# Reordering the last eight row blocks of a one-core graph-attention and layer-norm kernel

## The chip, the cores and the metric

The kernel runs on one core of a Trainium2 chip. The metric is the device time of one execution in microseconds. Six runs of the kernel before took 236.86 to 239.29 us, with a median of 237.13.

## The reference

`x` has 4096 rows of 512 numbers, `adj` 4096 rows of 4096, and `W` maps 512 features to 4 heads of 512. With the head count H = 4, what is computed is:

```
ht      = (x @ W) split into heads
e       = leaky_relu(src_i + dst_j) + adj[i, j]      for each head
h_prime = mean over heads of softmax_j(e) @ ht
out     = layernorm(x + h_prime)                     eps = 1e-5
```

The entries of `adj` reach 1e9 and most are zero, so in each row the largest entry leads by far more than the attention scores can make up. The softmax is then one at the column of that entry and zero elsewhere, and the row's result is `layernorm(x[i] + x[col(i)] @ mean of the heads' W)`. The kernel computes this, and beside it a test that every row's lead is large enough: a bound on the scores from the norms of x and of the weight vectors, compared with the gap between the largest and the second largest entry. The number of rows that fail is counted; if it is not zero, a general path follows, which these inputs don't enter.

## The kernel before

The rows are handled in 32 blocks of 128 (NB = 32), row `p * 32 + ib` being partition p of block ib. `BEHIND` is 24, `LATE` is 28, `KB` is 4 (512 features in four parts of 128). The order of the work is written out by hand: each engine executes its instructions in the order in which the program issues them, and the framework adds the semaphore waits between engines.

For each block the steps are:

- SyncE's queue loads the block's adjacency (2 MB). VectorE reduces it to 64 segment maxima (L163) and finds the largest segment (L170, L172). GpSimd fetches that segment with an indirect DMA (L176). VectorE finds the column in it (L192, L198), and GpSimd gathers the rows of x at these columns (`gather_rows`, L186). For block 31 VectorE searches the whole adjacency row instead (`find_column_in_row`, L206, 128 x 4096).
- `turn`: TensorE transposes the gathered rows in four parts into PSUM (L213), and ScalarE copies them to SBUF as `yt` (L215).
- `residual` adds the block's own rows of x to the PSUM accumulator through a product with the identity (L221). `products(ib, lo, hi)` adds the products of parts lo to hi-1 with the mean weights (L228). An fp32 product shows in the profile as two passes.
- The layer norm has two forms. `stats`, `rstd` and `finish`: two passes with sums on ScalarE (L250, L252), three small operations on GpSimd (L255 to L257) and a scaling on ScalarE (L261). Or `moments`, `factor` and `normalise`: VectorE takes mean and variance (L281, L285), ScalarE the root (L287), VectorE the reciprocal (L290; with `shift` also minus mean times reciprocal, L292) and the scaling (L297). `finish` can follow `factor` with `shift`.
- `row_norm`: ScalarE sums the squares of the block's x (L235), for the bound.

In the loop over the blocks these steps overlap. Blocks 24 to 27 are treated apart: their products alone are copied to a buffer (`put_by`, L241), and x is added later (`add_x`, L244, on GpSimd or VectorE), because their x is loaded only after the last adjacency. Block 31 is worked in two halves of 256 columns with an accumulator each (`residual_in_halves` L266, `products_of_half` L270, `stats_of_half` L304, `finish_in_halves`).

What follows the loop, L456 to L522, is the end of the kernel, and is what the change rewrites. In it stand, in the order of the program: the row norms of the last blocks; the stores of finished blocks; the column search of 30 and 31; the x of 24 to 27; residual, products and norm of 28 to 31; and the test. The test is `bound(0)` (the largest row norm `xm` on VectorE, L367, turned into a row by TensorE, L369), `bound(1)` (its maximum `xg`, L371, and root on ScalarE, L372), `bound(2)` (spread over the partitions by TensorE, L375), `bound(3)` and `test` (eight small VectorE operations, L377 to L390), `count` (a product with ones on TensorE, L394) and `report` (three VectorE operations, L398 to L401). `find_inner` (L192) takes the eight largest of a fetched segment.

The part of the end that sets the order between TensorE and VectorE reads:

```python
    residual(LATE)
    products(LATE, KB - 1, KB)
    residual_in_halves(NB - 1)
    turn(NB - 3)
    residual(NB - 3)
    products(NB - 3, 0, KB - 1)
```

Of the kernel before, what the change touches and what calls it, by code (L numbers as in the profile page):

```python
# [66 lines left out]
def leading_rows(ctx, tc, x, adj, W, a, out, ident, v, n_bad, any_bad):  # L67
# [141 lines left out]
    def turn(ib):  # L209
        y = y_t.pop(ib)  # L210
        tp = psum.tile([P, KB, P], F32, name="tp", bufs=2)
        for kb in range(KB):
            nc.tensor.transpose(tp[:, kb, :], y[:, ts(kb, P)], ident)  # L213
        yt = yt_of[ib] = rows.tile([P, KB, P], F32, name="yt")
        nc.scalar.copy(yt, tp)  # L215

    def residual(ib):
        start = ib not in o_ps
        if start:
            o_ps[ib] = psum.tile([P, D], F32, name="o")  # L220
        nc.tensor.matmul(o_ps[ib], ident, hold[:, ib, :], start=start, stop=False)  # L221

    def products(ib, lo=0, hi=KB):
        start = ib not in o_ps
        if start:
            o_ps[ib] = psum.tile([P, D], F32, name="o")
        for kb in range(lo, hi):
            nc.tensor.matmul(  # L228
                o_ps[ib], yt_of[ib][:, kb, :], w_sum[:, kb, :],
                start=(start and kb == 0), stop=(kb == KB - 1),  # L230
            )

    def row_norm(ib):
        sq = rows.tile([P, D], F32, name="sq")
        nc.scalar.activation(sq, hold[:, ib, :], AF.Square, accum_out=xx[:, ib : ib + 1])  # L235
# [7 lines left out]
    def add_x(engine, ib):  # L243
        engine.tensor_add(hold[:, ib, :], hold[:, ib, :], o_ps["by"][:, ib - BEHIND, :])  # L244
        o_ps[ib] = hold[:, ib, :]

    def stats(ib):
        o, i = o_ps[ib], slice(ib, ib + 1)
        sq = rows.tile([P, D], F32, name="sq")
        nc.scalar.activation(sq, o, AF.Identity, scale=-1.0 / D, accum_out=nm[:, i])  # L250
        sq = rows.tile([P, D], F32, name="sq")
        nc.scalar.activation(sq, o, AF.Square, bias=nm[:, i], accum_out=sd[:, i])  # L252
# [6 lines left out]
    def finish(ib):  # L259
        i = slice(ib, ib + 1)  # L260
        nc.scalar.activation(hold[:, ib, :], o_ps.pop(ib), AF.Identity, bias=nm[:, i], scale=sd[:, i])  # L261

    def residual_in_halves(ib):
        o_ps[ib] = [psum.tile([P, D // 2], F32, name="o") for _ in range(2)]
        for k, o in enumerate(o_ps[ib]):
            nc.tensor.matmul(o, ident, hold[:, ib, ts(k, D // 2)], start=True, stop=False)  # L266
# [10 lines left out]
    def moments(ib):  # L277

        if ib < NB - 1:
            st = small.tile([P, nc.vector.BN_STATS_DIM], F32, name="st", bufs=2)  # L280
            nc.vector.bn_stats(st, o_ps[ib])  # L281
        else:
            st = halves_st
        mv = mean_var[ib] = small.tile([P, nc.vector.BN_AGGR_DIM], F32, name="mv", bufs=3)
        nc.vector.bn_aggr(mv, st)  # L285
        r = rt[ib] = sd[:, ib : ib + 1]
        nc.scalar.activation(r, mv[:, 1:2], AF.Sqrt, bias=eps)  # L287
# [8 lines left out]
    def normalise(ib, o, columns=slice(0, D)):  # L296
        nc.vector.tensor_scalar(  # L297
            hold[:, ib, columns], o, mean_var[ib][:, 0:1], rt[ib], op0=OP.subtract, op1=OP.mult
        )
# [63 lines left out]
    def bound(part):  # L363

        if part == 0:
            xm = once.tile([P, 1], F32, name="xm")
            nc.vector.tensor_reduce(xm, xx, axis=AX.X, op=OP.max)  # L367
            px = of_bound[0] = psum.tile([1, P], F32, name="px", bufs=1)
            nc.tensor.transpose(px, xm, ident)  # L369
        elif part == 1:  # L370
            nc.vector.tensor_reduce(xg, of_bound[0], axis=AX.X, op=OP.max)  # L371
            nc.scalar.activation(xg, xg, AF.Sqrt)  # L372
        elif part == 2:
            pb = of_bound[2] = psum.tile([P, 1], F32, name="px", bufs=1)
            nc.tensor.matmul(pb, ones[0:1, :], xg, start=True, stop=True)  # L375
        else:
            nc.vector.tensor_mul(lead_by, of_bound[2], vn)  # L377
            nc.vector.tensor_scalar(lead_by, lead_by, 1.05, 110.0, op0=OP.mult, op1=OP.add)
# [3 lines left out]
    def test():  # L382
        a1 = top[:, :, 0]
        nc.vector.tensor_tensor(gap, top[:, :, 1], inner[:, :, 1], op=OP.max)
        size = once.tile([P, NB], F32, name="size")
        nc.vector.scalar_tensor_tensor(size, a1, -1.0, a1, op0=OP.mult, op1=OP.max)
        nc.vector.tensor_sub(gap, a1, gap)
        nc.vector.tensor_scalar(size, size, -(2.0 ** -22), lead_by, op0=OP.mult, op1=OP.subtract)
        nc.vector.scalar_tensor_tensor(gap, gap, 0.9999, size, op0=OP.mult, op1=OP.add)
        nc.vector.tensor_scalar(gap, gap, 0.0, None, op0=OP.is_gt)  # L390

    def count():
        pg = psum.tile([1, NB], F32, name="px", bufs=1)
        nc.tensor.matmul(pg, ones[:, 0:1], gap, start=True, stop=True)  # L394
        return pg
# [57 lines left out]
            finish(t - FINISH)  # L453
            finish(t - FINISH + 1)

    for ib in range(BEHIND, LATE + 2):  # L456
        row_norm(ib)
    for ib in range(0, 2 * Q, Q):
        store(nc.sync, ib, Q)
# [1 line left out]
        store(nc.sync, ib, 2)  # L461
    find_column(NB - 2)
    add_x(nc.gpsimd, BEHIND)
    add_x(nc.gpsimd, BEHIND + 1)
    find_column_in_row(NB - 1)
    add_x(nc.gpsimd, BEHIND + 2)
    residual(LATE)
    products(LATE, KB - 1, KB)
    residual_in_halves(NB - 1)
    turn(NB - 3)  # L470
    residual(NB - 3)
    products(NB - 3, 0, KB - 1)
    row_norm(NB - 2)
    row_norm(NB - 1)
    moments(LATE)
    for ib in range(BEHIND, NB):
        find_inner(ib)
    bound(0)
    products(NB - 3, KB - 1, KB)
    stats(BEHIND)  # L480
    factor(LATE)
    normalise(LATE, o_ps.pop(LATE))
    bound(1)
    turn(NB - 2)
    bound(2)
    add_x(nc.vector, LATE - 1)
    stats(BEHIND + 1)
    moments(LATE - 1)
    products(NB - 2, 0, 2)
    bound(3)  # L490
    test()
    pg = count()
    products(NB - 2, 2, KB - 1)
    stats(BEHIND + 2)
    rstd(slice(BEHIND, BEHIND + 2))
    rstd(slice(BEHIND + 2, BEHIND + 3))
    moments(NB - 3)
    report(pg)
    turn(NB - 1)
    factor(LATE - 1, shift=True)  # L500
    factor(NB - 3)
    normalise(NB - 3, o_ps.pop(NB - 3))
    finish(BEHIND)
    finish(BEHIND + 1)
    products(NB - 2, KB - 1, KB)
    products_of_half(NB - 1, 0)
    products_of_half(NB - 1, 1)
    nc.vector.tensor_add(hold[:, NB - 2, :], o_ps[NB - 2], hold[:, NB - 2, :])
    o_ps[NB - 2] = hold[:, NB - 2, :]
    moments(NB - 2)  # L510
    stats_of_half(NB - 1, 0)
    factor(NB - 2)
    normalise(NB - 2, o_ps.pop(NB - 2))
    finish(BEHIND + 2)
    finish(BEHIND + 3)
    stats_of_half(NB - 1, 1)
    moments(NB - 1)
    factor(NB - 1, shift=True)
    finish_in_halves(NB - 1)
    for ib, n in ((NB - 4, 1), (NB - 3, 1), (BEHIND, 2), (NB - 2, 1), (BEHIND + 2, 2)):  # L520
        store(nc.sync, ib, n)
    store(nc.sync, NB - 1, 1)  # L522

# [152 lines left out]
```

## Time and profile before

| what | value |
|---|---|
| median of six runs | 237.13 us |
| the profiled execution | 237.11 us |
| its span | 235.6 us |
| TensorE busy | 198.5 us, 84% |
| VectorE busy | 186.6 us, 79% |
| ScalarE busy | 111.7 us, 47% |
| GpSimd busy | 101.3 us, 43% |
| DMA | 97.73 MB, mean 415 GB/s |
| VectorE, segment maxima (L163) | 68 instructions, 146.0 us |
| TensorE, products (L228) | 248 passes, 117.0 us |
| TensorE, residuals (L221) | 52 passes, 28.5 us |

The span is the time from the first to the last instruction of the program; what the measured time has beyond it, 1.5 us here, lies around it. Shares of busy time are averages over the whole span. They say little of the end of the kernel, where the adjacency has arrived and a few engines hand work to one another: there the chain of waits, the timeline and the windows are to be read. In a line of the timeline the first number is the start, the second the busy time, then engine, line, operation, what it writes from what, and in brackets the idle time before it and what ended that.

### The profile page before, as it was taken

What the parts mean: (1) busy time and instruction counts of PE and PEld (TensorE: products, weight loads), DVE (VectorE), ACT (ScalarE), POOL (GpSimd) and SP (SyncE); (2) the same over time, 40 slices, a digit from 0 to 9 for tenths busy, and PEclk for the clock granted to TensorE, in tenths of its full rate; (3) what the DMA queues carried; (4) which work ended last, traced back from release to release, by engine and by line L of the source; (5) the groups of instructions that cost most, each with busy time, mean ns of one, the idle gap of its engine ahead of it and who ended that gap; (6) DMA issues with size and microseconds to landing.
All of it is one profiled execution on the core that took longest, in us unless ns stands there. A gap on an engine that the chain in (4) does not pass through costs nothing.

```text
span 235.6 us, 2500 instructions
## 1 busy us (share of the span) xinstructions
PE 198.5 (84%) x683; PEld 102.8 (44%) x683; DVE 186.6 (79%) x302; ACT 111.7 (47%) x267; POOL 101.3 (43%) x215
## 2 busy tenths in 40 slices
PE   0198959999999999999959999697899968799990
PEld 0034526456656556656434443242443433245460
DVE  2735875589869995999579979898799899989772
ACT  2002012155757557474726464546464645137782
POOL 1112232415427462646352655464365564548130
PEclk9999799999999999999985999999799999999999
DMA  6999999999999999999999999999999999999995
GB/s 232 436 441 410 445 417 440 415 440 417 431 436 410 429 428 446 420 420 440 417 431 437 420 437 423 430 417 433 426 439 411 419 426 419 419 423 420 417 361 214
DMA packets 13697, 97.73 MB, mean 415 GB/s; under 512 B 2152, under 2 KB 2152, under 8 KB 7792
## 3 DMA queue, kind: packets, MB, share of 16 engines
q1 hardware_dynamic: 10080, 88.08, 88.6%
q0 software_dynamic: 3584, 9.44, 10.1%
q8 instruction: 6, 0.10, 0.2%
q14 instruction: 11, 0.09, 0.1%
q10 hardware_dynamic: 16, 0.02, 0.0%
HBM read 89.15 MB, written 8.39 MB: 414 GB/s over the span
## 4 chain that ended last, share of the span: by engine, by line
POOL 33%; issue 33%; DMA 18%; PE 9%; DVE 3%; POOLq 1%; ACT 1%; SPq 1%
DMA adj_t<-in_adj_dram 15%; POOL lead L176 11%; POOL y L186 10%; PE o L228 5%; POOL sd L256 4%; DMA y<-in_x_dram,col 3%; POOL start L181 2%; POOL col L200 2%; POOL row L174 2%; DVE seg L163 2%; PE o L270 2%; POOL sd L255 1%; POOL nm L257 1%; PE tp L213 1%; PE o L221 1%
## 5 line engine op out<-in xcount | busy, mean ns | idle before, releaser
L163 DVE TENSOR_REDUCE seg<-adj_t 128x32 f32<-128x2048 f32 (+1 forms) x68 | 146.0, 2150 | 35.1 <-DMA adj_t<-in_adj_dram 34.6
L228 PE MATMUL o<-w_sum,yt 128*128 128x512 f32 x248 | 117.0, 612 | 1.0 <-ACT yt L215 1.0
L228 PEld LDWEIGHTS o<-w_sum,yt 128*128 128x128 f32 x248 | 45.4, 194 | 56.1 <-issue 44.5
L215 ACT COPY yt<-tp 128x512 f32<-128x512 f32 x32 | 18.8, 588 | 46.7 <-PE tp L213 43.9
L176 POOL DMA_INDIRECT lead<-in_adj_dram,row x32 | 32.3, 1010 | 14.2 <-POOL row L174 14.2
L186 POOL DMA_INDIRECT y<-in_x_dram,col x32 | 30.9, 965 | 16.0 <-POOL col L200 15.5
L318 PE MATMUL o<-hold,ident 128*128 128x512 f32 x32 | 18.9, 745 | 15.2 <-DMA hold<-in_L_gnn_W_dram 15.2
L213 PE MATMUL tp<-ident,y 128*128 128x128 f32 x128 | 20.3, 283 | 11.8 <-DMA y<-in_x_dram,col 11.8
L221 PE MATMUL o<-hold,ident 128*128 128x512 f32 x52 | 28.5, 631 | 0.5 <-DMA hold<-in_x_dram 0.5
L213 PEld LDWEIGHTS tp<-ident,y 128*128 128x128 f32 x128 | 15.1, 145 | 24.7 <-issue 23.5
L200 POOL TENSOR_TENSOR col<-start,within 128x1 uint32<-128x1 uint32 x31 | 5.9, 190 | 45.5 <-DVE within L198 45.5
L336 ACT COPY wt<-tp 128x512 f32<-128x512 f32 x16 | 9.2, 587 | 32.3 <-PE tp L334 27.7
L174 POOL TENSOR_TENSOR row<-at,first 128x1 uint32<-128x1 uint32 x32 | 6.1, 189 | 39.3 <-DVE at L172 39.3
L235 ACT ACTIVATE sq<-hold 128x512 f32<-128x512 f32 x32 | 19.8, 619 | 0.0
L342 PEld LDWEIGHTS pv<-at_d,wt 128*128 128x128 f32 x128 | 16.3, 191 | 6.8 <-ACT wt L336 3.5
L318 PEld LDWEIGHTS o<-hold,ident 128*128 128x128 f32 x32 | 7.3, 239 | 24.5 <-POOL row L174 11.1
L319 ACT ACTIVATE w_sum<-o 128x512 f32<-128x512 f32 x4 | 2.4, 598 | 31.5 <-PE o L318 31.5
L261 ACT ACTIVATE hold<-o,nm,sd 128x512 f32<-128x512 f32 x24 | 17.2, 770 | 0.0
L252 ACT ACTIVATE sq<-o,nm 128x512 f32<-128x512 f32 x24 | 16.5, 687 | 0.8
L342 PE MATMUL pv<-at_d,wt 128*128 128x2 f32 x128 | 15.3, 244 | 0.6 <-ACT wt L336 0.6
L250 ACT ACTIVATE sq<-o 128x512 f32<-128x512 f32 x24 | 14.6, 607 | 0.0
L334 PEld LDWEIGHTS tp<-ident,hold 128*128 128x128 f32 x64 | 7.9, 142 | 6.9 <-issue 6.9
(85 smaller groups left out, 138.2 us busy)
## 6 DMA issues: line engine op xcount, KB each, us to landing
adj_t<-in_adj_dram SPq DMA_DIRECT2D x27, 2048.0 KB, 32.5
hold<-in_x_dram SPq DMA_DIRECT2D x7, 1024.0 KB, 31.6
adj_t<-in_adj_dram SPq DMA_DIRECT2D x6, 1024.0 KB, 30.7
out_dram<-hold SPq DMA_DIRECT2D x10, 512.0 KB, 11.9
adj_t<-in_adj_dram SPq DMA_DIRECT2D x8, 512.0 KB, 13.6
hold<-in_L_gnn_W_dram SPq DMA_DIRECT2D x4, 1024.0 KB, 8.2
out_dram<-hold SPq DMA_DIRECT2D x2, 1024.0 KB, 15.7
hold<-in_x_dram SPq DMA_DIRECT2D x2, 512.0 KB
```

Source lines behind the costliest of these rows:

```text
L163: nc.vector.tensor_reduce(seg_of[ib][:, ts(k, S // n)], adj_t[ib][:, ts(k, N // n)].rearrange("p (s e) -> p s e", e=E), axis=AX.X, op=OP.max,)
L176: nc.gpsimd.indirect_dma_start(out=lead, out_offset=None, in_=adj_segs, in_offset=bass.IndirectOffsetOnAxis(ap=row[:, :1], axis=0),)
L186: nc.gpsimd.indirect_dma_start(out=y, out_offset=None, in_=x, in_offset=bass.IndirectOffsetOnAxis(ap=col[:, :1], axis=0),)
L213: nc.tensor.transpose(tp[:, kb, :], y[:, ts(kb, P)], ident)
L215: nc.scalar.copy(yt, tp)
L221: nc.tensor.matmul(o_ps[ib], ident, hold[:, ib, :], start=start, stop=False)
L228: nc.tensor.matmul(o_ps[ib], yt_of[ib][:, kb, :], w_sum[:, kb, :], start=(start and kb == 0), stop=(kb == KB - 1),)
L235: nc.scalar.activation(sq, hold[:, ib, :], AF.Square, accum_out=xx[:, ib : ib + 1])
L252: nc.scalar.activation(sq, o, AF.Square, bias=nm[:, i], accum_out=sd[:, i])
L261: nc.scalar.activation(hold[:, ib, :], o_ps.pop(ib), AF.Identity, bias=nm[:, i], scale=sd[:, i])
L318: nc.tensor.matmul(o, ident, hold[:, w_at + kb * H + h, :], start=(h == 0), stop=(h == H - 1))
L342: nc.tensor.matmul(pv[:, kb, h : 2 * H : H], wt[:, k, :], at_d[:, k, h : 2 * H : H], start=(k == 0), stop=(k == KB - 1),)
```

## The change

The end of the kernel is rewritten in its order, and two steps change their engine:

- Block 28 has no residual on TensorE. VectorE adds its x to the finished products, with a new function `add_x_to_products`, which block 30 already had written out.
- Block 26 has its mean and variance from VectorE (`moments`, and `factor` with `shift`) instead of ScalarE and GpSimd (`stats`, `rstd`). GpSimd adds block 26's x before block 25's, and both after the gather of block 31.
- Turn 29 is issued before the half residuals of 31. Turn 30 is issued before residual 29 and the last product of 29, turn 31 after the first product of 30 and before the other three.
- The steps of the bound, the test and the count stand at other places among these. The maxima of the fetched segments are taken in two groups of four. Row norm 29 follows the copy of turn 29.
- The x of block 27 is added after the report, with its moments later still.
- The store of blocks 26 and 27 is issued ahead of block 30's.
- The tile `mv` has six buffers instead of three.

Four lines are added ahead of the end, so its line numbers in the changed kernel are higher by four than those above.

```diff
+    def add_x_to_products(ib):
+        nc.vector.tensor_add(hold[:, ib, :], o_ps[ib], hold[:, ib, :])
+        o_ps[ib] = hold[:, ib, :]
...
-        mv = mean_var[ib] = small.tile([P, nc.vector.BN_AGGR_DIM], F32, name="mv", bufs=3)
+        mv = mean_var[ib] = small.tile([P, nc.vector.BN_AGGR_DIM], F32, name="mv", bufs=6)
...
-    for ib in range(BEHIND, LATE + 2):
+    for ib in range(BEHIND, LATE + 1):
         row_norm(ib)
...
     find_column(NB - 2)
     add_x(nc.gpsimd, BEHIND)
-    add_x(nc.gpsimd, BEHIND + 1)
     find_column_in_row(NB - 1)
     add_x(nc.gpsimd, BEHIND + 2)
-    residual(LATE)
+    add_x(nc.gpsimd, BEHIND + 1)
     products(LATE, KB - 1, KB)
+    turn(NB - 3)
     residual_in_halves(NB - 1)
-    turn(NB - 3)
-    residual(NB - 3)
     products(NB - 3, 0, KB - 1)
-    row_norm(NB - 2)
-    row_norm(NB - 1)
+    for ib in range(LATE + 1, NB):
+        row_norm(ib)
+    add_x_to_products(LATE)
     moments(LATE)
-    for ib in range(BEHIND, NB):
+    stats(BEHIND)
+    moments(BEHIND + 2)
+    bound(0)
+    for ib in range(BEHIND, LATE):
         find_inner(ib)
-    bound(0)
-    products(NB - 3, KB - 1, KB)
-    stats(BEHIND)
     factor(LATE)
     normalise(LATE, o_ps.pop(LATE))
+    factor(BEHIND + 2, shift=True)
+    turn(NB - 2)
     bound(1)
-    turn(NB - 2)
+    residual(NB - 3)
     bound(2)
-    add_x(nc.vector, LATE - 1)
+    products(NB - 3, KB - 1, KB)
+    for ib in range(LATE, NB):
+        find_inner(ib)
     stats(BEHIND + 1)
-    moments(LATE - 1)
-    products(NB - 2, 0, 2)
+    rstd(slice(BEHIND, BEHIND + 2))
     bound(3)
     test()
+    products(NB - 2, 0, 1)
     pg = count()
-    products(NB - 2, 2, KB - 1)
-    stats(BEHIND + 2)
-    rstd(slice(BEHIND, BEHIND + 2))
-    rstd(slice(BEHIND + 2, BEHIND + 3))
+    finish(BEHIND + 2)
+    turn(NB - 1)
     moments(NB - 3)
     report(pg)
-    turn(NB - 1)
-    factor(LATE - 1, shift=True)
+    add_x(nc.vector, LATE - 1)
     factor(NB - 3)
     normalise(NB - 3, o_ps.pop(NB - 3))
     finish(BEHIND)
     finish(BEHIND + 1)
-    products(NB - 2, KB - 1, KB)
+    moments(LATE - 1)
+    products(NB - 2, 1, KB)
     products_of_half(NB - 1, 0)
     products_of_half(NB - 1, 1)
-    nc.vector.tensor_add(hold[:, NB - 2, :], o_ps[NB - 2], hold[:, NB - 2, :])
-    o_ps[NB - 2] = hold[:, NB - 2, :]
+    factor(LATE - 1, shift=True)
+    finish(LATE - 1)
+    add_x_to_products(NB - 2)
     moments(NB - 2)
     stats_of_half(NB - 1, 0)
     factor(NB - 2)
     normalise(NB - 2, o_ps.pop(NB - 2))
-    finish(BEHIND + 2)
-    finish(BEHIND + 3)
     stats_of_half(NB - 1, 1)
...
-    for ib, n in ((NB - 4, 1), (NB - 3, 1), (BEHIND, 2), (NB - 2, 1), (BEHIND + 2, 2)):
+    for ib, n in ((NB - 4, 1), (NB - 3, 1), (BEHIND, 2), (BEHIND + 2, 2), (NB - 2, 1)):
         store(nc.sync, ib, n)
```

## The prediction

> **What bounds the kernel now.** I read four views in this order. First the page's second part: the DMA row is full from the second slice to the last but one, so the body streams the adjacency at the DMA's speed. The change touches nothing there; only what follows the last adjacency rows, from about 209 us, can move. Second the chain of waits over that stretch, because it tells which engine sets the end:
>
> ```profile
> 209.42 0.63 PE tp L213 x4
> 210.05 3.57 PE o L228 x8
> 213.62 0.86 PE o L221 x2
> 214.48 0.86 PE o L228 x2
> ...
> 221.58 0.02 issue
> 221.60 0.59 ACT yt L215
> 222.20 0.04 issue
> 222.24 1.99 PE o L228 x4
> ...
> 226.73 3.55 PE o L270 x16
> 230.28 0.02 issue
> 230.30 0.44 DVE halves_st L304
> ```
>
> Columns: start, length, what. From 209.42 to 230.28 the chain stays on TensorE but for one stop of 0.65 us, the copy of block 30's turned rows at 221.60. Each 512-wide fp32 product or residual is two passes, 0.86 us. After 230.30 comes a serial tail of moments, root, reciprocal, scaling and last store, which the change leaves alone.
>
> Third the timeline of GpSimd and VectorE there, for the operations that are moved:
>
> ```profile
> 211.37 4.42 DVE L206 FIND_INDEX8 col<-top,adj_t 128x8 uint32<-128x4096 f32 x1
> ...
> 213.56 2.51 POOL L244 TENSOR_TENSOR hold<-hold,adj_t 128x512 f32<-128x512 f32 x2
> ...
> 216.55 0.97 POOL L186 DMA_INDIRECT y<-in_x_dram,col  x1 [0.48 <-issue]
> 217.54 1.28 POOL L244 TENSOR_TENSOR hold<-hold,adj_t 128x512 f32<-128x512 f32 x1
> ...
> 218.53 0.18 DVE L367 TENSOR_REDUCE xm<-xx 128x1 f32<-128x32 f32 x1 [0.93 <-ACT sq L235]
> ...
> 219.99 0.27 PE L369 MATMUL px<-ident,xm 128*1 128x128 f32 x1
> ```
>
> The gather of block 31 cannot start before VectorE's search ends at 215.79; the add of block 26's x (L244 at 217.54) stands behind that gather on GpSimd. Fourth the one-microsecond windows: DMA moves about 418 GB/s up to 226 us and 201 to 432 after it, so the last stores run almost at the DMA's pace too. The (26,27) store is issued at 230.2 and takes 3.4 us to land.
>
> [...] all of these rows run in the written order. [...] the add from PSUM (L508) took 692. [...] normalise took 0.81 from PSUM and 0.55 from SBUF.
>
> **The change, part by part.** Line numbers are those of before.
>
> 1. Block 28's residual leaves TensorE: minus 2 passes, 0.86 us on the chain. Its add goes to VectorE, 0.69 + 0.04 us, right after the search, where VectorE had 0.93 us idle before xm; its normalise now reads SBUF, 0.26 shorter.
> 2. Turn 29 is ahead of the two half residuals (4 x 0.215 = 0.86), which hide the 0.59 us copy as residual 29 did. It would start at 214.32; the queue's wait for gather 29 ended at 214.1, so 0.2 us of cover is left. Products 29 (three, six passes) then run 215.61 to 218.26 instead of 217.34 to 219.99. So far TensorE is 1.7 us ahead.
> 3. GpSimd: gather 31 no longer waits for the second add. Search end 215.79, release 0.04, then 0.27 to 0.51 as the other gathers show: start 216.10 to 216.34, take 216.22 (before 216.55). Add 26 follows: 217.21 to 218.49. Add 25 moves behind it, to 219.8; its readers on ScalarE come at 221.5.
> 4. Block 26's moments move to VectorE (0.73 + 0.18) and **add a wait**: VectorE stands at 217.33 and waits for add 26 until 218.53. Queued behind it: xm, four maxima, block 28's scaling, all of the bound. Moments end at 219.4, xm runs 219.35 to 219.53 (the 218.53 it had was a wait for row norms, which now end at 217.6). ScalarE loses the two passes of 26 (1.56 us) and GpSimd one rstd (about 1.1); both had idle time, so nothing is won there.
> 5. TensorE reaches the first bound product (L369) at 218.26 and waits for xm until 219.60: **1.34 us idle**, because turn 30, residual 29 and product 29 stand behind it. Turn 30 starts at 219.73 (before 220.96); gather 30 was issued at 212.57 and took 6.7 us, so it is there at 219.3. Its copy (0.65 with waits) is now hidden by residual 29, which ends at 221.03.
> 6. Second bound product: VectorE after xm does four maxima (4 x 0.126), reciprocal 28, normalise 28 (0.55 + 0.2), factor 26 (0.35), then xg at 220.93, 0.28; ScalarE's root to 221.43; product at 221.47. TensorE idle 0.44 us. Then product 29 and one of 30, 221.75 to 223.54, while VectorE's maxima and test (1.28 after the product's end at 221.87) end at 223.2: no wait at count. Count at 223.54 (before 224.15).
> 7. Turn 31 at 223.69 (before 225.27). Gather 31 is due at 216.22 + 6.7 = 222.9. Behind it now stand three products of 30 (6 x 0.4285 = 2.57) and the halves: 223.69 + 0.43 + 2.57 = 226.70, halves 16 passes, 226.70 + 15 x 0.2155 + 0.38 = 230.31 (before 230.26). The copy of 31 (0.59) is hidden by the products.
> 8. VectorE's tail: report, add 27 (0.67), scaling 29 (0.81), moments and factor of 27, add and moments of 30 (0.69, 0.69, 0.18), first half's moments (0.43), scaling 30 (0.55). Laid end to end with ScalarE's roots between, scaling 30 ends at 230.5 to 230.75 (before 229.65), so the second half's moments start then, against 230.30: **plus 0.2 to 0.45 us**. ScalarE's finish of 24 to 27 is done by 228.8.
> 9. Stores: (26,27) goes ahead of 30, issued near 228.8 instead of 230.2; 30 near 230.7 instead of 229.7. Both precede the last, issued near 232.7 (before 232.32). Three more mv buffers add no instruction: nothing.
>
> Sum on TensorE: minus 0.86 (residual), minus about 0.4 (wait for copy 30 that showed as idle), plus 1.34 and 0.44 of new idle time; minus about 0.45 of what the first bound product, turn 30, second product and count had lost to their own starts: about zero. VectorE's tail adds 0.2 to 0.45, middle 0.35. The profiled execution took 237.11 us with a span of 235.6; the median of the runs is 237.13, the same. Predicted: 237.13 + 0.35 = 237.5 us.
>
> Unknown costs. Gather 31's dispatch: 0.12 us either side, one for one. Landing of gathers: 6.7, 6.8 in this stretch, median 7.9 and longest 9.5 over the run; below 7.4 it is free. GpSimd's add beside VectorE's work: 1.28 in all three rows; I take it, with 1.2 and 1.5 as bounds. Moments of 26 gain if ScalarE's relief reaches the tail; the finish of 27 is before the last scaling anyhow, so between 0 and minus 0.2.
>
> **The rivals.** *A (likeliest, 0.70):* as above; with its bounds minus 0.3 to plus 1.0, so 236.8 to 238.1.
>
> *B, the wait at the first bound product is small and the end moves up (0.17).* For it: TensorE's work really shrinks by 0.86 plus the 0.37 us idle before 222.24, which would end the halves at 229.0. Against: the search, gather, add, moments order is fixed by three FIFO queues. Even then the gain is cut: the (26,27) store landed at 230.2 + 3.4 = 233.6 behind stores that were queued, and 0.25 MB more take 0.6 us at 418 GB/s, so the last store can hardly land before 234.2; it now lands about 1 us before the span's end, at 234.6. Gain 0.4: 236.7 us.
>
> *C, slower: gather 31 lands late (0.13).* Turn 31 was at 225.27, 8.7 us after its gather's issue; now it is at 223.69, 7.5 after, and 2.57 us of block 30's products stand behind it on the in-order TensorE. Any landing beyond 7.4 us delays the end one for one. At the longest of this trace, 9.5, that is 2.0 on top of 0.35: 239.5 us. Against it: the two gathers nearest in time took 6.7 and 6.8.
>
> That the change doesn't do what it says is not likely: by the queues, bound, count and copy of 31 do come sooner (0.4, 0.6 and 1.6 us by my schedule); what does not come sooner is the end.
>
> **How the numbers follow.** About 1%, 2.4 us, is what a measurement of this kernel can tell from no change (its own six runs lie between 236.86 and 239.29). A and B are wholly within it. C passes it only at its far end. With the runs' own spread of 2.4 us upwards: faster 0.02, same 0.88, slower 0.10. The range takes B's 236.7 and A with its bounds, and part of C: 236.6 to 238.9, leaving out about 0.15.
>
> **What would show it.** VectorE's wait of about 1.2 us ended by GpSimd's add, before a 128x512 moments; TensorE idle more than 1 us before the first bound product; turn 31 near 223.7; last half product ending near 230.3; a second-half moments start at 230.5 or later, with scaling 30 just before it. I am wrong if that first wait is under 0.5 us, if turn 31 waits for its gather, or if the last store's issue is before 232.

## The result and the profile after

| | before | after |
|---|---|---|
| median of all runs | 237.07 us (71 runs, 236.56 to 239.71) | 238.46 us (33 runs, 237.73 to 239.41) |
| ratio to before, 95% interval | 1 | 1.0038 (1.002 to 1.0055) |
| profiled execution | 237.11 us | 237.93 us |
| its span | 235.6 us | 236.4 us |
| last store issued | 232.32 | 232.50 |
| its last part landed after the issue | 2.31 us | 2.94 us |

The trace records 16 landings for the last store, called its parts here, from 1.84 to 2.31 us after the issue in before and from 1.85 to 2.94 in after. The ratio compares fast executions and is what the text goes by (the medians alone stand 0.6% apart): 0.38% of 237.1 us is 0.9 us, with 0.5 to 1.3 as its interval. That is slower, by less than the 1% that counts as a change here, and within the predicted range. The predicted 0.4 us (237.5 against 237.13) lies just under the interval.

The timeline of after, in the stretch where before was read (start, length, engine, line, operation, and in brackets the idle time ahead of it with what ended it):

```profile
211.03 4.42 DVE L206 FIND_INDEX8 col<-top,adj_t 128x8 uint32<-128x4096 f32 x1
...
216.21 0.96 POOL L186 DMA_INDIRECT y<-in_x_dram,col  x1 [1.96 <-issue]
...
218.51 0.69 DVE L285 BATCH_NORM_STATS2 st<-hold 128x6 f32<-128x512 f32 x1 [1.52 <-POOL hold L244]
...
219.54 0.27 PE L373 MATMUL px<-ident,xm 128*1 128x128 f32 x1 [1.51 <-DVE xm L371]
...
221.39 0.29 PEld L379 LDWEIGHTS px<-xg,ones 1*128 1x128 f32 x2 [0.78 <-ACT xg L376]
221.39 0.38 PE L379 MATMUL px<-xg,ones 1*128 1x1 f32 x2
...
223.76 0.66 PE L213 MATMUL tp<-ident,y 128*128 128x128 f32 x4
```

The new wait is there: VectorE stands 1.52 us until GpSimd's add of block 26 ends, and TensorE behind it 1.51 us until xm. The second bound product itself shows no idle time, but its weight load (PEld) waited for ScalarE's root, which was done at 221.33. Turn 31 is at 223.76. The search of block 31, 215.79 at its end before, ended at 211.03 + 4.42 = 215.45 here. That is 0.34 us sooner with nothing changed ahead of it; times of the two traces are therefore compared from the search's end too. The gather of 31 starts at 216.21, which is 0.76 after that end. Before, it was 216.55 - 215.79 = 0.76 as well.

The chain of waits of after (start, length, what):

```profile
217.20 1.28 POOL hold L244
218.48 0.02 issue
218.51 0.70 DVE st L285
219.21 0.02 issue
219.24 0.18 DVE mv L289
219.42 0.08 DVE xm L371
219.50 0.04 issue
219.54 0.28 PE px L373
219.83 0.12 issue
219.95 0.63 PE tp L213 x4
...
229.92 0.55 DVE hold L301
230.47 0.02 issue
230.48 0.44 DVE halves_st L308
```

Where before had TensorE alone, the chain now runs GpSimd's add, VectorE's moments, xm, the bound product, turn 30. At its end the second half's moments (L308, at 230.48) follow directly on the scaling of block 30 (L301) instead of the last product. The last product ended at 230.45, so TensorE and VectorE come to the end together. From the search's end the moments stand at 230.48 - 215.45 = 15.03, against 230.30 - 215.79 = 14.51 before: the computation ends 0.52 us later. That is no chance of one execution: the same two figures come back in e4 and e5 below (15.03, the arithmetic of after) and in e6 and e8 (14.51, that of before). On the traces' own clocks the last store goes out only 0.18 later, since this execution's search was 0.34 sooner.

The other 0.63 us of the spans' difference lie **behind the last instruction of the kernel's arithmetic**. The DMA rate over 3.2 us from the issue of the last store, in 40 slices of 80 ns, first before, then after:

```profile
GB/s 307 52 103 0 102 0 102 51 51 0 179 384 410 410 410 410 384 410 205 77 0 205 0 0 0 0 0 0 0 0 0 0 0 0 0 0 0 0 0 0
```

```profile
GB/s 51 51 51 51 0 0 0 0 0 0 179 333 486 384 384 358 384 358 231 52 102 0 26 26 51 26 26 26 26 26 0 0 0 0 0 0 0 0 0 0
```

The bulk moves in the same slices, 0.8 to 1.5 us after the issue. The single 205 of before, at 1.7 us, is two 8 KB packets. Then after shows eight slices at 26 to 51 GB/s, to 2.4 us, where before is empty: a few engines are still at work. The completions agree: 14 of the 16 parts of the store land by 1.98 us after its issue in both, the last two at 2.26 and 2.31 before and at 2.89 and 2.94 after.

What else goes over the DMA engines there? The program ends with `flag = nc.values_load(any_bad[0:1, 0:1], ...)` (L61) and a branch on it, in every engine's instruction stream. Of the queues, the "instruction" one moves two packets of 8 KB in this stretch, in both traces. The loads of the flag, on VectorE's and ScalarE's sequencers (shortest, median, longest in ns, then start in us), first before, then after:

```profile
L61 DVEq TENSOR_LOAD <-any_bad x1: 806/806/806, 231.5 to 231.5; - x1
L61 ACTq TENSOR_LOAD <-any_bad x1: 656/656/656, 231.7 to 231.7; - x1
```

```profile
L61 DVEq TENSOR_LOAD <-any_bad x1: 537/537/537, 231.7 to 231.7; - x1
L61 ACTq TENSOR_LOAD <-any_bad x1: 477/477/477, 231.9 to 231.9; - x1
```

Both start 0.77 and 0.58 us ahead of the last store's issue in both kernels. In before the loads end 0.04 and 0.07 us after it, in after 0.23 and 0.11 us ahead of it. The two 8 KB packets on the instruction queue, called fetches here, follow the loads: at 1.70 and 1.71 us after the issue in before, at 1.02 and 1.64 in after, where the first took 766 ns instead of 309. That the branch brings them about is the author's reading; the traces show the order alone. Why are the loads shorter in after? The one-microsecond windows (stretch, its length, the five engines' busy times, then TensorE's clock, DMA share and GB/s), before and then after:

```profile
231.00:232.00 1.00, 0.00 (x0) 0.00 (x0) 0.63 (x3) 0.57 (x2) 0.00 (x0) 1.00 1.07 432
232.00:233.00 1.00, 0.00 (x0) 0.00 (x0) 0.15 (x1) 0.29 (x1) 0.00 (x0) 1.00 0.49 201
```

```profile
231.00:232.00 1.00, 0.00 (x0) 0.00 (x0) 0.60 (x4) 0.38 (x2) 0.00 (x0) 1.00 0.73 287
232.00:233.00 1.00, 0.00 (x0) 0.00 (x0) 0.33 (x1) 0.48 (x1) 0.00 (x0) 1.00 0.12 45
```

In before the (26,27) store, issued at 230.2, keeps the DMA at 432 GB/s from 231 to 232, while the flag is loaded. In after that store went out at 228.69 and that of block 30 alone at 230.49, so the DMA drains before the last store comes: 287 GB/s in the first window, 45 in the second. **Theory:** an idle DMA gives a short load, an early branch, and fetches that meet the last store. **Rival:** the loss is in the arithmetic's order (the new wait and VectorE's tail), and the landing is chance.

### The profile page after: what moved, and what is told of

Its sections match the earlier page's. It is cut to its first block, busy times and chain, and to the rows that moved or that the text cites. A ratio compares the mean times of both kernels' runs of the same rounds, so it can differ in the third digit from the quotient of the medians.

```text
span 236.4 us, 2495 instructions
## 1 busy us (share of the span) xinstructions
PE 198.2 (84%) x681; PEld 102.6 (43%) x681; DVE 187.7 (79%) x307; ACT 110.8 (47%) x264; POOL 100.2 (42%) x212
## 4 chain that ended last, share of the span: by engine, by line
POOL 32%; issue 30%; DMA 16%; PE 15%; DVE 3%; ACT 1%; POOLq 1%; SPq 0%
DMA hold<-in_L_gnn_W_dram 11%; POOL lead L176 10%; POOL y L186 10%; PE o L228 7%; POOL sd L260 3%; DMA y<-in_x_dram,col 3%; PE o L322 2%; DMA adj_t<-in_adj_dram 2%; POOL start L181 2%; POOL col L200 2%; PE pv L346 2%; POOL row L174 2%; PE tp L213 2%; PE o L221 1%; POOL hold L244 1%
## 5 line engine op out<-in xcount | busy, mean ns | idle before, releaser
L228 PE MATMUL o<-w_sum,yt 128*128 128x512 f32 x248 | 115.0, 606 | 0.7 <-ACT yt L215 0.7
L322 PE MATMUL o<-hold,ident 128*128 128x512 f32 x32 | 20.9, 813 | 14.8 <-DMA hold<-in_L_gnn_W_dram 14.8
L221 PE MATMUL o<-hold,ident 128*128 128x512 f32 x50 | 27.4, 631 | 0.0
L322 PEld LDWEIGHTS o<-hold,ident 128*128 128x128 f32 x32 | 8.1, 264 | 25.3 <-POOL row L174 11.0
L254 ACT ACTIVATE sq<-o 128x512 f32<-128x512 f32 x24 | 14.6, 608 | 0.0
```

The lines of the kernel that those rows point to most:

```text
L228: nc.tensor.matmul(o_ps[ib], yt_of[ib][:, kb, :], w_sum[:, kb, :], start=(start and kb == 0), stop=(kb == KB - 1),)
L322: nc.tensor.matmul(o, ident, hold[:, w_at + kb * H + h, :], start=(h == 0), stop=(h == H - 1))
```

## The experiments

Kernels of one batch shared a chip and its runs of before: (e1, e2, e3, e5), (e4, e7, e8, e9), (e6, e11, e12, e13). Ratios are to before.

**e1: the wait that holds the bound back.** In after, xm and the four maxima go ahead of block 26's moments.

```diff
-    moments(BEHIND + 2)
     bound(0)
     for ib in range(BEHIND, LATE):
         find_inner(ib)
+    moments(BEHIND + 2)
```

> The changed kernel with one step moved: the largest row norm xm and four of the maxima go ahead of block 26's moments on VectorE. Theory 1 (VectorE's wait for GpSimd's add of block 26 holds back xm, and with it TensorE): TensorE's idle time before the first bound product falls from 1.5 us to about 0.1, but gather 30, which landed at 219.8, then ends the wait before turn 30, so TensorE still idles 0.8 to 1.5 us there and the kernel gains no more than 0.3 us on the changed one. Rival (VectorE's tail sets the end, TensorE has slack): idle time moves in the same way and the end doesn't move at all, within 0.2 us of the changed kernel. Rival (the wait alone is the whole loss): the kernel falls by 0.9 us or more, to the kernel before.

Measured: 1.0052 (1.0034 to 1.007). The 1.51 us of idle time before the first bound product is gone, but the kernel is no faster for it. TensorE then waited 0.31 us for gather 30, 0.93 before the second bound product and, as its timeline shows, for gather 31:

```profile
225.54 0.63 PE L213 MATMUL tp<-ident,y 128*128 128x128 f32 x4 [0.18 <-DMA y<-in_x_dram,col]
```

From the search's end, the last half product ended after 14.62 us instead of 15.0: the 1.5 us of waiting was worth 0.4. The last part of the last store landed 3.38 us after its issue, more than in after.

**e2: e1, and block 29 finished ahead of turn 30.**

```diff
-    turn(NB - 2)
-    bound(1)
     residual(NB - 3)
-    bound(2)
     products(NB - 3, KB - 1, KB)
+    turn(NB - 2)
+    bound(1)
+    bound(2)
```

> As the run before, and residual 29 and the last product of 29 go ahead of turn 30 again, which fills the time in which TensorE would wait for gather 30. Theory 1: no idle time over 0.4 us on TensorE between 218 and 220; the halves' last product ends near 229.3 instead of 230.4, and the second half's moments start at 229.9 to 230.4, then bound by VectorE. Time 0.3 to 0.8 us under the changed kernel. Rival (VectorE's tail): the last product ends a microsecond earlier and the time stays within 0.2 us of the changed kernel. Rival (the last store is what was lost): the time depends on where the store's issue falls against the instruction fetch, and does not follow TensorE.

Measured: 1.0057 (1.0033 to 1.0082). The waits moved again (0.20 us for gather 30, 0.77 before the second bound product, 0.35 before the count), the end stayed at 14.6. The store landed after 3.14 us. Neither order of TensorE's queue repairs the loss.

**e3: block 28's x on VectorE alone, in before.**

```diff
-    residual(LATE)
...
+    nc.vector.tensor_add(hold[:, LATE, :], o_ps[LATE], hold[:, LATE, :])
+    o_ps[LATE] = hold[:, LATE, :]
     moments(LATE)
```

> The kernel before with one part of the change: block 28's x is added on VectorE and its residual leaves TensorE; all else stands as before. Theory 1 (TensorE's work sets the end of the kernel before): the last product ends 0.7 to 0.9 us sooner than 230.26, VectorE's second-half moments start near 229.6, and the time falls by 0.4 to 0.8 us under the kernel before. Rival (the stores' DMA sets the end): the last product ends as much sooner, but the last store lands no more than 0.4 us sooner. Rival (VectorE is the bound): no gain, since the add costs it 0.7 us.

Measured: 1.0003 (0.9981 to 1.0025). The profile shows the residual's 0.86 us: from the start of turn 28 the halves end after 20.11 us instead of 20.84, and the last store goes out after 22.17 instead of 22.89. But one of its parts landed late, 2.77 us after the issue, so 0.46 of the 0.73 us are given back there. Contrary to what the expectation of e9 says below, no fetch stands ahead of that part: its 2 KB packets run on until 2.17 us after the issue, and a fetch starts at 2.18. The (26,27) store's own last part had landed only 1.89 us after that issue.

**e5: more engine work behind the last store, in after.** One 128x512 copy on ScalarE and one 128x512 add on VectorE, whose results nothing reads, were to hold the branch back.

```diff
+    nc.scalar.copy(rows.tile([P, D], F32, name="sq"), w_sum[:, 0, :])
+    nc.vector.tensor_add(rows.tile([P, D], F32, name="wt"), w_sum[:, 1, :], w_sum[:, 2, :])
```

> The changed kernel with work added: after their last instruction ScalarE copies 128x512 once more and VectorE adds 128x512 once more, into buffers that nothing reads, so that their branch to the program's end comes 0.6 us later. Theory of the fetch (in the profiled run of the changed kernel an instruction fetch of 8 KB on the DMA engines starts 0.2 us after the last store's first packets and holds back a part of them by 0.7 us; before, it starts after them): the last store lands about 2.3 us after its issue instead of 2.9, and the kernel gets faster by 0.3 to 0.6 us although it does more. Rival (the fetch is chance, or of no weight): the time stays the same or grows by up to 0.6 us.

Measured: 1.005 (1.003 to 1.007). The loads didn't move: they again start 0.77 and 0.58 us ahead of the store's issue and take 0.54 and 0.47. The fetches came 1.04 and 1.05 us after the issue and took 829 and 756 ns, and the store landed after 3.35 us. VectorE's sequencer loads the flag at 232.3, while its engine still has operations queued: VectorE is busy for 0.88 us of the window from 232 to 233 and for 0.50 us of the next. So the edit failed in its purpose and told something else: the work added at the end did not delay the load, nor the fetches after it.

**e4: before's order of the last stores, in after.**

```diff
-    for ib, n in ((NB - 4, 1), (NB - 3, 1), (BEHIND, 2), (BEHIND + 2, 2), (NB - 2, 1)):
+    for ib, n in ((NB - 4, 1), (NB - 3, 1), (BEHIND, 2), (NB - 2, 1), (BEHIND + 2, 2)):
```

> The changed kernel with the stores in the order of the kernel before: block 30's ahead of that of 26 and 27. In the profiles the last store's slowest two parts land 2.3 us after its issue in the kernel before and 2.9 to 3.4 us in the changed one and those made from it, and ahead of that the loads of the count on ScalarE and VectorE take 0.65 and 0.81 us before, 0.48 and 0.54 after, so that their branch comes 0.2 to 0.25 us sooner against the last store. Theory S (the store order is why: 26 and 27 no longer keep the DMA busy while the count is loaded): the loads take 0.65 to 0.8 us again, the last part lands within 2.8 us of its issue, and the kernel is 0.3 to 0.7 us under the changed one. Rival (something else sets the branch, the order costs nothing): loads and landing as in the changed kernel, same time.

Measured: 1.0006 (0.9979 to 1.0033). The arithmetic ends as in after, 14.99 us after the search. But block 30's store is ready late and the larger one now waits behind it, so the DMA is busy while the flag is loaded (397 and 389 GB/s in the windows 232 to 234), and the loads are long:

```profile
L61 DVEq TENSOR_LOAD <-any_bad x1: 1121/1121/1121, 232.4 to 232.4; - x1
L61 ACTq TENSOR_LOAD <-any_bad x1: 1054/1054/1054, 232.6 to 232.6; - x1
```

They end 0.35 and 0.47 us behind the issue (233.22), and the last part lands 2.00 us after it. With more bytes shortly ahead of it the last store landed sooner, after 2.00 us instead of 2.94.

**e7: the branch made to wait, in after.** Two one-column operations, each with something to wait for: VectorE copies a column of ScalarE's last result, ScalarE copies that. Only scratch is written.

```diff
+    nc.vector.tensor_copy(late[:, 0:1], hold[:, NB - 1, D - 1 :])
+    nc.scalar.copy(late[:, 1:2], late[:, 0:1])
```

> The changed kernel with two operations of one column added at the end, VectorE's waiting for ScalarE's last scaling and ScalarE's for that, so that their branch really comes later, by 0.5 to 0.8 us. (In the run with one more copy and one more add the branch had not moved: it was taken before that work was done.) Theory of the fetch: the two 8 KB fetches start later than 1.6 us after the last store's issue, its last part lands within 2.5 us of it, and the kernel is 0.5 to 0.9 us faster than the changed one. Rival (the slow parts are slow for another reason, as the two DMA engines that lag in all stores): landing 2.9 us or more, and no gain.

Measured: 1.0016 (0.9988 to 1.0043). Now the loads start after the last store's issue, and are short:

```profile
L61 DVEq TENSOR_LOAD <-any_bad x1: 539/539/539, 234.1 to 234.1; - x1
L61 ACTq TENSOR_LOAD <-any_bad x1: 472/472/472, 234.3 to 234.3; - x1
```

The fetches start at 1.81 and 1.82 us, when the store's packets are through, and the last part lands 1.98 us after the issue. The semaphore waits held back the loads and, with them, the fetches; e5's added work had not (0.77 and 0.58 us ahead of the issue, 1.04 and 1.05 behind it). This kernel's profiled execution took 238.91 us, above its median of 238.04, for a reason told at the end.

**e8: the same two operations in before; e9: in e3.**

> The kernel before with the same two operations. Theory of the fetch: in its profile the fetches already come after the store's packets, so at most 0.2 us are won in the mean, from runs in which they don't. Rival: no difference, or slower by up to 0.2 us for the later end of the two engines.

> The kernel before with block 28's x on VectorE alone, and the two operations at the end. With block 28 alone, the last store was issued 15.5 us after the search of block 31, a microsecond sooner than before, and landed 0.5 us sooner, one part of it late behind a fetch. Theory of the fetch: that part lands within 2.4 us, and the kernel is 0.6 to 1.1 us faster than the kernel before. Rival (the DMA's drain of the stores holds the landing): no better than block 28 alone, within 0.3 us.

Measured: 0.9988 (0.9965 to 1.0011) and 0.999 (0.9968 to 1.0012). Both land 1.99 us after the issue (2.31 in before, 2.77 in e3). Side by side, e7 and e8 have the landing alike and differ by the rest of the change, the arithmetic's order above all: 0.0028 of 237 is 0.7 us, in one batch, though their intervals overlap, and e7's profiled execution has a slower stretch of TensorE in it, told at the end. e9 against e8 asks what block 28's residual is worth once landing is equal. The profile has the last product 0.4 us sooner from the search's end (14.09 against 14.47), and the times show nothing. Counted from the start of turn 28, which waits for a gather of its own, the halves end after 19.98 us against 20.84: the residual's 0.86 us is there.

**e6: after's order of the last stores, in before.**

```diff
-    for ib, n in ((NB - 4, 1), (NB - 3, 1), (BEHIND, 2), (NB - 2, 1), (BEHIND + 2, 2)):
+    for ib, n in ((NB - 4, 1), (NB - 3, 1), (BEHIND, 2), (BEHIND + 2, 2), (NB - 2, 1)):
```

> The kernel before with one part of the change: the store of 26 and 27 is issued ahead of block 30's. There the two stores are ready within half a microsecond of each other (block 30 at 229.7, 26 and 27 at 230.2), so the DMA is as busy up to the last store as before. Theory S (what counts is whether the DMA is busy while ScalarE and VectorE load the count, since that sets how late they branch and fetch): loads of 0.65 us or more, last part landed within 2.6 us of the issue, and the time within 0.15% of the kernel before. Rival (the order itself costs): 0.2 to 0.4% slower.

Measured: 0.9973 (0.9949 to 0.9997). The order as such does no harm. In before the (26,27) store isn't ready until about 230.2, so with either order the DMA is busy as the flag is loaded: 1.10 and 0.93 us, last part 1.97 us after the issue. By this reading, what costs in after is that the larger store is done with too early.

**e11: GpSimd's add of 26 ahead of gather 31.** In e4.

```diff
+    add_x(nc.gpsimd, BEHIND + 2)
     find_column_in_row(NB - 1)
-    add_x(nc.gpsimd, BEHIND + 2)
```

> The changed kernel with the stores in the order of before, and GpSimd's add of block 26 ahead of the gather of 31, so that VectorE's moments of 26 don't wait. The run with the store order alone was at 1.0006 of the kernel before. Theory 1 (the wait on VectorE costs in the end): VectorE's wait of 1.5 us is gone, xm comes 1.1 us sooner, TensorE's idle time before the first bound product is under 0.4 us, but turn 30 then waits for gather 30; the last product ends 0.2 to 0.5 us sooner, and the time is 0.998 to 1.000 of the kernel before. TensorE's clock stays whole from 205 to 233 us. Rival (TensorE's idle time has slack behind it): no sooner end of the last product, time as with the store order alone.

Measured: 0.998 (0.9959 to 1.0). VectorE's wait for the add of 26 and TensorE's before the first bound product are gone, and the gather starts 0.84 us after the search's end instead of 0.76. TensorE now waits 0.60 us for gather 30 ahead of turn 30, and 0.43 for gather 31. The chain of e11 shows what bounds next:

```profile
214.61 1.22 POOL hold L244
215.83 0.16 issue
215.99 7.06 DMA y<-in_x_dram,col
223.05 0.14 issue
223.19 0.64 PE tp L213 x4
...
229.32 0.55 DVE hold L301
229.87 0.02 issue
229.88 0.44 DVE halves_st L308
```

Turn 31 waits for its gather, 7.06 us, and behind it VectorE's tail ends with the scaling of 30 as in after. The last product ends 14.70 us after the search. Together with e4 this undoes after's wait and its late landing, and the rest of the change is worth nothing that can be told from before.

**e12: e11, block 29 finished ahead of turn 30 as in e2, and the second half's moments ahead of block 30's scaling.**

```diff
+    residual(NB - 3)
+    products(NB - 3, KB - 1, KB)
     turn(NB - 2)
     bound(1)
-    residual(NB - 3)
     bound(2)
-    products(NB - 3, KB - 1, KB)
...
-    normalise(NB - 2, o_ps.pop(NB - 2))
     stats_of_half(NB - 1, 1)
     moments(NB - 1)
+    normalise(NB - 2, o_ps.pop(NB - 2))
```

> As the run before, and two steps moved: residual 29 and the last product of 29 ahead of turn 30, and the second half's moments of 31 ahead of the scaling of block 30 on VectorE. Theory 1 with VectorE's tail as the next bound: the halves' last product ends 20.3 us after turn 28 starts or sooner (21.4 in the changed kernel, 20.9 before), the second half's moments follow it within 0.3 us instead of waiting for the scaling of 30, and the time is 0.993 to 0.998 of the kernel before. Rival (the stores' drain): last product and last scaling come sooner, the last part of the last store does not, time 0.998 to 1.002.

Measured: 1.0065 (1.0043 to 1.0086), the slowest of all. From its timeline:

```profile
230.54 0.43 DVE L308 BATCH_NORM_STATS2 halves_st<-o 128x6 f32<-128x256 f32 x1 [0.60 <-PE o L274]
...
231.13 0.49 DVE L301 TENSOR_SCALAR hold<-hold,mv,sd 128x512 f32<-128x512 f32 x1
...
231.65 1.31 SPq L317 DMA_DIRECT2D out_dram<-hold  x3
```

The moments wait for the products again, as meant, but the scaling of 30 is now at 231.13. Its store and the (26,27) behind it go out from 231.65, within 0.9 us of the last at 232.56. The DMA is at 0 GB/s in the window 231 to 232, and at 428 and 383 in 233 to 235. Even the last store's first part landed only after 2.82 us, and its last after 3.91. Nor did the arithmetic gain: TensorE waited 0.77 us before the second bound product and 0.35 before the count, the last product ended 14.96 us after the search (14.70 in e11), and the last store was issued 17.02 us after it (16.76 in e11). A step that feeds a store was put off for nothing.

**e13: e9, and turn 30 ahead of the last product of 29.**

```diff
-    products(NB - 3, KB - 1, KB)
...
     turn(NB - 2)
+    products(NB - 3, KB - 1, KB)
```

> The kernel before with block 28's x on VectorE, the two waiting operations at the end, and turn 30 ahead of the last product of 29, which then hides the copy of 30. Without that last step the run was at 0.999. Theory 1: no idle time on TensorE between turn 30 and block 30's products (0.4 us there before), the last product ends 19.6 us after turn 28 starts, and the time is 0.994 to 0.998 of the kernel before. Rival (gather 30 lands too late for it, or the drain of the stores holds the landing): 0.998 to 1.001.

Measured: 0.9989 (0.9971 to 1.0008). From the search's end the last product ended after 13.68 us, 0.8 sooner than in e8. One part of the last store landed late (2.49 us; here its packets end at 1.90, as a fetch starts), and the time is that of e8 and e9. What takes these 0.4 to 0.8 us back in e9 and e13 isn't settled; the intervals, down to 0.9968 and 0.9971, don't rule out that most of it was won. Their searches ended 0.2 to 0.3 us later than e8's on the traces' clocks, which is less than executions differ among themselves.

Two of the quantities, over all fourteen kernels:

| flag loads end, from the last store's issue | kernels | last part lands after | ratio |
|---|---|---|---|
| 0.24 to 0.11 us ahead of it | after, e1, e2, e5, e12 | 2.94 to 3.91 us | 1.0038 to 1.0065 |
| 0.04 to 0.68 us behind it | before, e3, e4, e6, e7, e8, e9, e11, e13 | 1.97 to 2.77 us | 0.9973 to 1.0016 |

There is no kernel between the groups; e12 has stores queued ahead as well. e4 and e7 moved after from the upper row to the lower by two unlike edits. Each of their intervals overlaps after's, so for one of them alone the gain could be chance. Taken together, after and e5 (the same arithmetic and order of stores) stand at 1.0043 and e4 and e7 at 1.0011; an estimate from their four intervals, taken as independent, puts the difference at 0.0032, with 0.0023 either side.

The records give the landing of one execution of each kernel, and they don't name the engine that carried a packet, but the packets' times speak for the fetch. In e2 the two fetches end 1.75 and 1.79 us after the issue of the last store, and the last store's remaining 16 packets of 2 KB, two parts of it, begin at 1.75 and 1.78. In e1 the fetches end at 1.75 and 1.90 and these packets begin at 1.75 and 1.90, in e5 at 1.81 and 1.87 and at 1.80 and 1.87. In after the fetches end at 1.79 and 1.95, and nine packets follow from 1.79 on. In before the fetches start, at 1.70 and 1.71, when the store's packets are through. That engines simply run late is a rival: in after, two parts of block 30's store lag too, landing up to 0.73 us after the last store's issue. But in e7 one part of that store lags to 0.63 us, and all 16 parts of the last store are in by 1.98.

Two things stay open. One is why, in e1, two parts had not begun before a fetch that started only at 1.44 us. The other is what makes a load long. In VectorE's and ScalarE's loads length and traffic go together (0.65 us and more with the DMA at 415 GB/s or above during the load, 0.54 or less at 257 and below). But the sequencers of GpSimd and TensorE load the same word earlier, and in after they took 0.51 us at 224.35 and 0.49 at 225.99, in the midst of 414 to 418 GB/s. A busy DMA is thus not the whole condition.

No kernel beats before clearly: e6 (0.9973) and e11 (0.998) have intervals that end at 0.9997 and 1.0.

## Why the prediction was right, and where its size was off

**The direction and the wait were right (parts 1, 2, 4, 5).** VectorE waited 1.52 us (1.2 predicted), TensorE 1.51 (1.34). The bound product came at 219.54 (219.60), turn 30 at 219.95 (219.73), where gather 30 had only just landed, 7.84 us after its issue instead of 6.7. That the clock times agree so well is luck in part: they were worked out from a search that ends at 215.79, and in this execution it ended 0.34 us sooner. From the search's end the bound product came after 4.09 us, and 3.81 was forecast.

**Part 3 was wrong in its reason, and its term was mis-sized.** "Gather 31 no longer waits for the second add" was to win 0.33 us. It hadn't waited for it: it starts 0.76 us after the search in both traces, though the adds ahead of it ended at 216.07 before and at 214.25 after, and 0.76 us in every other kernel but e11. The 216.21 that matches the forecast comes from the early search. The release-to-dispatch time of the other gathers was taken from the GpSimd operation ahead of them; here VectorE releases. The prediction allowed 0.12 us either side for it, "one for one"; it was 0.33 us more, and the add of 26 duly ended 3.03 us after the search instead of 2.70. It is the first link of a chain that ended 0.48 us later than forecast (part 7).

**Part 6 had the second wait, with a slip in its sum.** VectorE's operations as listed end at 221.13, not 220.93: the reciprocal's 0.2 us is left out. They overlap in the run and took 1.35 us from xm's end to xg, so the slip did no harm. In after the wait for ScalarE's root is covered by the late turn 30. In e4 and e5, where gather 30 was in time, TensorE waits 0.26 and 0.25 us there (0.44 predicted), and in all three the second bound product comes 5.93 to 5.94 us after the search (5.68 predicted).

**Part 7 was late by as much.** The count at 223.61 (223.54), turn 31 at 223.76 (223.69) and the halves' end at 230.45 (230.31) agree on the clock by the same luck. From the search's end the halves end after 15.00 us, where 14.52 was forecast and before has 14.47: the sum on TensorE was "about zero" and measured 0.53. Gather 31 landed 7.05 us after its issue, below the 7.4 at which rival C begins but over the 6.7 and 6.8 taken from "the two gathers nearest in time" (gather 29 of before, issued at 206.97 and landed at 214.05, had needed 7.1); in e1 and e11, with turn 31 sooner after the search, it did decide.

**Part 8 was near.** Scaling 30 ended at 230.47 (230.5 to 230.75) and the second half's moments began at 230.48, plus 0.18 on the clock for a forecast of 0.2 to 0.45. From the search's end it is 0.52. VectorE's tail was to be what ends later; TensorE's last product is as late.

**Part 9 is the largest term that was mis-sized.** It named the stores' new times rightly, (26,27) at 228.69 (228.8), 30 at 230.49 (230.7), the last at 232.50 (232.7), and priced what follows at nothing, as it did the serial tail which "the change leaves alone". The landing of the last store grew by 0.63 us. The arithmetic's 0.52 and this 0.63 make 1.15 us in the two profiled executions, for 0.9 (0.5 to 1.3) measured over the runs. The change took the (26,27) store away from the time at which the flag is loaded; e4 and e7 put the delay back in two ways, and most of the excess is gone (1.0006 and 1.0016, with the overlap told above).

**Rival B's cap** was on the right resource with the wrong sign. It argued that stores queued ahead would hold the last one up. e12 shows that this exists, when two are issued within 0.9 us of it. In after fewer were ahead of it, and it landed later.

## What to carry to other kernels

Look behind the last instruction: compare how long the last store takes to land in two kernels, and what else the DMA moves then. When a wait is removed from one engine's path, write down the next floor before counting the gain: here it was the search's end + 0.8 + a gather of 7.06 us in e11, which gave back most of 1.5 us of idle time. And count the start of a released operation from the event that released it, not from the one ahead of it in its queue.

## What the runs showed of the hardware

- A sequencer's load of one word took 0.47 to 0.54 us in most cases and 0.65 to 1.12 us when it fell among the last stores (0.81 and 0.66 in before, 1.12 and 1.05 in e4). Earlier loads by GpSimd and TensorE stayed short at 414 to 418 GB/s (0.51 and 0.49 us in after).
- In eight of the fourteen kernels the first fetch starts 1.25 to 1.30 us after VectorE's load of the flag ends (1.26 in after; in before it is 1.66). Where a fetch came ahead of the last parts of a store, they began when it ended (in e2 the fetches end 1.75 and 1.79 us after the issue, these packets begin at 1.75 and 1.78).
- Sequencers loaded the flag while their engines still had operations to do (in after, VectorE's load starts at 231.74, its last scaling at 231.80). Added work didn't move the load (e5: 0.77 us ahead of the last store's issue, as in after), a semaphore wait did (e7: behind it, at 234.1).
- The gather of 31 on GpSimd, which VectorE's search releases, started 0.76 us after the search's end in thirteen kernels (0.84 in e11). Where an operation of GpSimd released a gather, it took 0.27 us (gather 30 in before and after), 0.39 (gather 29 in before) or 0.42 (gather 30 in e4).
- What stood behind a waiting operation in its engine's queue waited too. In after the last row norm ended at 216.98, but xm ran at 219.33, behind the moments of 26 and their wait of 1.52 us; in e1, with xm ahead of them, TensorE's 1.51 us of idle time before the first bound product were gone.
- On 128x512 an add took 1.28 us on GpSimd and 0.67 on VectorE (L244, before). VectorE's add with one operand in PSUM took 692 ns in before (L508) and 671 to 683 in after (L248), its scaling 0.81 us from PSUM and 0.55 from SBUF (L297, before).
- TensorE's granted clock fell after short idle time; between 190 and 230 us it did so in one trace alone. In e7's profiled execution TensorE was idle 1.28 and 0.52 us between 217.9 and 219.97, with only the 0.27 us of the bound product between, and then (after the five busy times, the clock is the third number from the end):

```profile
220.00:221.00 1.00, 1.00 (x5) 0.76 (x6) 0.96 (x7) 0.33 (x1) 0.00 (x0) 0.71 1.02 418
221.00:222.00 1.00, 1.00 (x2) 0.00 (x0) 0.25 (x2) 0.97 (x5) 0.00 (x0) 0.50 1.02 414
222.00:223.00 1.00, 1.00 (x4) 0.72 (x4) 0.11 (x1) 1.00 (x3) 0.11 (x1) 0.50 1.03 414
223.00:224.00 1.00, 1.00 (x2) 0.48 (x3) 0.92 (x7) 0.51 (x1) 0.87 (x2) 0.58 1.03 418
```

  A residual took 1.71 us there instead of 0.86, and the last product ended 2 us later after the search than in after. After itself, with 1.51 us of idle time, keeps 1.00 through these windows. The traces show how near it was. In before and after, the stretches at one clock are 3.41 us long or multiples of it, but for the one that the end cuts off (3.41 and 6.83 us at half speed, 3.41 to 92.16 at full), and in the 3.41 us ahead of the drop in e7 (217.0 to 220.4) TensorE was busy for 47%, in the like step of after (218.0 to 221.4) for 52%. Between 40 and 230 us the fourteen traces hold 29 such drops, and all but one follow a step in which TensorE was busy for 8 to 47%; the four of before and after follow steps of 39, 31, 33 and 42%. The busy share alone doesn't settle it: ahead of 40 us the clock fell at 26.2 in before and at 26.9 in after, behind steps of 78 and 85%, and after kept full speed at 177.1 behind one of 47%. In e7 the drop is a cost of idle time on TensorE that no sum of waits has: 0.85 us on the residual alone. How often it comes in executions of after wasn't tried, so a share in the loss of the slower ones is not excluded.
